# A mixture of experts on lists of its own tokens, in a four-layer kernel on one core

## The chip, the core and the metric

The kernel runs on one NeuronCore of a Trainium2 chip. The metric is device time in microseconds of one execution, lower is better. All arithmetic is in 32-bit floats (some matmul operands are rounded to the fp32r format).

## The reference

Four residual layers on x of shape (4, 512, 128), that is four blocks (batch rows) of 512 tokens. Each layer normalizes its input (layer norm without gain) and adds its result to x.

```python
x = x + attention(ln(x), WQ, WK, WV, WO)     # 16 heads of 8, causal softmax
x = x + moe(ln(x), Wr, W1, b1, W2, b2)       # 8 experts, top 2
x = x + layer1(ln(x), ...)                   # gated linear recurrence and a feed-forward, layer norms inside
x = x + ternary(ln(x), w1, w2, h1, h2, w3)   # weights in {-1, 0, 1}, gelu between

def moe(x):
    xt = x.reshape(T, D)                               # T = 2048, D = 128
    topv, topi = top_k(softmax(xt @ Wr), 2)
    topv = topv / sum(topv)
    onehot = one_hot(topi, 8)
    rank = cumsum(onehot, axis=0)                      # over tokens, for each choice
    keep = (rank <= 320) * onehot                      # capacity int(T * 1.25 / 8)
    w = einsum('tk,tke->te', topv, keep)
    h = gelu(einsum('td,edf->etf', xt, W1) + b1)       # F = 512
    y = einsum('etf,efd->etd', h, W2) + b2
    return einsum('te,etd->td', w, y)
```

The reference computes all eight experts for all tokens and weighs them with w, which is zero for all but two experts of a token.

## The kernel before

A block's 512 tokens are four tiles of 128 (`TB` = 4). x is kept in SBUF as `xs` with tokens on partitions; matmuls take it transposed, `yT` (128 channels by 512 tokens). The stages are Python generators. Each yields after a step the time in us that the step is thought to take on TensorE, and `weave` (L158) merges several generators into one program order: it always continues the stage whose sum of yields, times a factor of the stream, is lowest. Matmuls and transposes (L62, L65) keep that order on TensorE, so a matmul whose operand is late holds up all that follow it there. On the other engines and queues the framework schedules instructions by itself, in an order that respects their dependencies; an engine executes its own list in order.

The work is two stretches a block, after an opening that does the attention of block 0 (L706 to L730). The first (L742 to L752) weaves `experts(b)` (factor 1.0), `feed(b-1)` and `ternary(b-1)` (1.2), and `maxima` of block b+1, the attention's row maxima (2.0); for b = 0, `round_weights`, which loads the ternary weights, rounds them on GpSimd and checks them, stands in for feed and ternary. For b = 4 only feed and ternary of the last block are left. The second (L755 to L763) weaves `recurrence(b)` (1.0) with a chain for the following blocks (0.8): the attention's second pass `second.group`, its `output`, `route(b+1)` and `project(b+2)`. `project` computes queries and keys, stores them to DRAM as `rows_q` and `rows_k` and loads them back spread as `qs` and `ks`, which `maxima` of the next stretch needs.

`route` (L351) computes the router's softmax and the two choices of each token (`oh`, one-hot by tile, choice and expert), counts ranks with matmuls against a triangular matrix (`pr`), applies the capacity, forms w, transposes it (`pw`), copies it (`wT`) and stores it to DRAM (`wd`).

`experts` (L441) runs each expert on all 512 tokens of the block. An expert is four matmuls of 512 columns into `ph`, a Gelu on ScalarE each (`hT`, L467), four matmuls into `py`, a product with the expert's row of w that a DMA has spread over all partitions (`wb`, L459; `yw`, L451), and on GpSimd a sum into `acc` (L452). The bias b2 enters by a matmul with w (`pb2`, L473). `second` of an expert is emitted within the next expert. At the end `acc` is transposed and added to `xs` (L481). `fetch` (L431) loads an expert's weights (`ew`) two experts ahead on the SP queue.

`recurrence` (L487) begins with two layer norms of `xs`, then a projection `pp` for each of 8 channel groups and four weights. `layernorm` (L111) takes four statistics on VectorE and a power on GpSimd (`ln_rs`, L122). In `ternary` (L580) `halves` (L581) splits an activation into a rounded and a residual half; the residual is computed on GpSimd for even indices and on VectorE for odd ones (L585). PSUM banks come from `bank` (L75): two with the tag "pt", shared by nearly all stages, and one "sum".

At the end a value that is nonzero when the ternary weights are not representable (`wide_weights`, L669) decides about a branch (L767) that recomputes the ternary layer in full precision. It is not taken with these inputs.

Of the kernel before, what the change touches and what calls it, by code (L numbers as in the profile page):

```python
# [10 lines left out]
F32 = mybir.dt.float32  # L11
F32R = mybir.dt.float32r
# [23 lines left out]
CAP = max(1, int(NB * S * 1.25 / E))  # L36

# [5 lines left out]
def block_kernel(ctx: ExitStack, tc: tile.TileContext, i: dict, out: bass.AP):  # L43
# [24 lines left out]
    class Turn:  # L68


        tile = ps_d.tile

    turn = Turn()

    def bank(name, tag="pt", shape=(P, S)):  # L75

        return ps_d.tile(list(shape), F32, tag=tag, name=name, bufs=2 if tag == "pt" else 1)
# [51 lines left out]
    def flip(src):  # L129

        pt = turn.tile([P, TB, P], F32, tag="pt", name="pt")
        for t in range(TB):
            transpose(pt[:, t, :], src[:, t, :])
        return pt
# [4 lines left out]
    def normed(src):  # L139
        y = ypool.tile([P, TB, D], F32, tag="y", name="y")  # L140
        layernorm(src, y)
        return y

    def turned(y, gain=None, shift=None):

        yT = ypool.tile([P, S], F32, tag="yT", name="yT", bufs=3)
# [38 lines left out]
    def project(b, big):  # L185
# [25 lines left out]
        pv = turn.tile([P, TB, D], F32, tag="pt", name="pv")  # L211
# [15 lines left out]
    def maxima(g):  # L227
# [27 lines left out]
        pm = turn.tile([P, TB, P], F32, tag="pt", name="pm")  # L255
# [8 lines left out]
    class Weights:  # L264
# [69 lines left out]
        def output(self, b):  # L334
# [6 lines left out]
            pa = turn.tile([P, TB, D], F32, tag="pt", name="pa")  # L341
# [6 lines left out]
    yTs, wTs, wds = {}, {}, {}  # L348
    taken = rt.tile([P, 2 * E], F32, name="taken")

    def route(b):  # L351
# [3 lines left out]
        yT = yTs[b] = turned(y)  # L355
        yield 1.0
        pl = turn.tile([P, TB, E], F32, tag="pt", name="pl")
# [19 lines left out]
        eq = rt.tile([P, TB, E], F32, name="rt_eq", tag="rt_eq")  # L377
        for k in range(2):
# [3 lines left out]
            first = rt.tile([P, TB], F32, name=f"rt_first{k}", tag=f"rt_first{k}")  # L382
            nc.vector.tensor_reduce(first, eq, AX.X, ALU.max)
            nc.vector.tensor_tensor(oh[:, :, k, :], revb, wide(first), ALU.is_equal)
# [13 lines left out]
        for t in range(TB):  # L398
# [6 lines left out]
        rank = rt.tile([P, TB, 2 * E], F32, name="rt_rank", tag="rt_rank")  # L405
        nc.vector.tensor_tensor(
            rank, pr[:, 0:TB, :], taken.unsqueeze(1).to_broadcast([P, TB, 2 * E]), ALU.add
        )
        nc.vector.tensor_tensor(taken, taken, pr[:, TB, :], ALU.add)
        wk2 = rt.tile([P, TB * 2, E], F32, name="rt_wk", tag="rt_wk")  # L410
        nc.vector.scalar_tensor_tensor(
            wk2.rearrange("p n e -> p (n e)"), rank.rearrange("p n k -> p (n k)"), CAP + 0.5,
            ohf.rearrange("p n k -> p (n k)"), ALU.is_le, ALU.mult,
        )
        nc.vector.tensor_tensor(wk2, wk2, wide(tv.rearrange("p n k -> p (n k)")), ALU.mult)
        w = rt.tile([P, TB, E], F32, name="rt_w", tag="rt_w")
        w4 = wk2.rearrange("p (n k) e -> p n k e", k=2)
        nc.vector.tensor_tensor(w, w4[:, :, 0, :], w4[:, :, 1, :], ALU.add)
        yield 3.0
        pw = turn.tile([E, TB, P], F32, tag="pt", name="pw")  # L420
        for t in range(TB):
            transpose(pw[:, t, :], w[:, t, :])
        wT = wTs[b] = rt.tile([E, S], F32, name="wT", tag="wT", bufs=2)
        nc.scalar.copy(wT, pw.rearrange("e t q -> e (t q)"))
        wd = wds[b] = scr.tile([E, S], F32, tag="wd", name="wd")
        nc.sync.dma_start(wd, wT)
# [4 lines left out]
    def fetch(n):  # L431

        if n < NB * E and n not in ews:
            e = n % E
            w1 = ew.tile([P, F], F32, tag="ew1", name="ew1")
            nc.sync.dma_start(w1, i["E1"][e])
            w2 = ew.tile([P, FC, D], F32, tag="ew2", name="ew2")
# [3 lines left out]
    def experts(b, moe):  # L441
        acc = moe.tile([P, S], F32, tag="acc", name="acc", bufs=1)
        late = None

        def second(e, hT, w2, wb):
            py = bank("py", "sum")
            for c in range(FC):
                mm(py, lhsT=w2[:, c, :], rhs=hT[c], start=(c == 0), stop=(c == FC - 1))
            yield 3.44
            yw = moe.tile([P, S], F32, tag="yw", name="yw")  # L450
            nc.vector.tensor_tensor(yw, py, wb, ALU.mult)  # L451
            nc.gpsimd.tensor_tensor(acc, acc, yw, ALU.add)  # L452

        for e in range(E):
# [3 lines left out]
            wb = moe.tile([P, S], F32, tag="wb", name="wb", bufs=2)  # L458
            nc.sync.dma_start(wb, wds[b][e : e + 1, :].to_broadcast([P, S]))  # L459
            fetch(n + 1)  # L460
            fetch(n + 2)
            hT = []
            for c in range(FC):
                ph = bank("ph")
                mm(ph, lhsT=w1[:, ts(c, P)], rhs=yTs[b], start=True, stop=True)
                h = moe.tile([P, S], F32, tag="hT", name="hT", bufs=6)
                nc.scalar.activation(h, ph, AF.Gelu, bias=mb1[:, e * FC + c : e * FC + c + 1])  # L467
                hT.append(h)
                yield 0.86
                if c == 1 and late is None:  # L470

                    pb2 = bank("pb2")
                    mm(pb2, lhsT=mb2, rhs=wTs[b], start=True, stop=True)  # L473
                    nc.vector.tensor_copy(acc, pb2)
                    yield 0.86
                elif c == 1:
                    yield from second(*late)
            late = (e, hT, w2, wb)
        yield from second(*late)
        yield 2.0  # L480
# [99 lines left out]
    def ternary(b, tern):  # L580
        def halves(src, hi, lo, c):  # L581

            nc.vector.tensor_copy(hi, src)  # L583
# [265 lines left out]
```

## Time and profile before

| | |
|---|---|
| device time, median of 3 runs | 934.65 us (932.77 to 938.14) |
| profiled execution, device time | 934.39 us |
| its span in the trace | 932.7 us |
| mean granted TensorE clock | 0.879 |
| TensorE matmul busy | 767.6 us, 82% |
| TensorE weight load busy | 357.8 us, 38% |
| VectorE busy | 410.8 us, 44% |
| ScalarE busy | 308.8 us, 33% |
| GpSimd busy | 173.2 us, 19% |
| DMA | 51.07 MB, mean 55 GB/s |

In the rows of the profile, PE is TensorE, PEld its weight loads, DVE is VectorE, ACT ScalarE, POOL GpSimd, and SPq the DMA queue of SyncE. A row of a group gives line, engine, operation, output and inputs, shapes and count, then busy time in us and the mean of one in ns, then the idle time of its engine ahead of it and what ended that. L63 and L66 are the helpers for all matmuls and transposes, so those rows are told apart by tile names. A 32-bit matmul appears as two records (two weight loads and two passes). Ends of matmuls are modelled, so the durations of consecutive ones overlap; the chain of waits shows how much time a run of them took.

### The profile page before, as it was taken

What the parts mean: (1) busy time and instruction counts of PE and PEld (TensorE: products, weight loads), DVE (VectorE), ACT (ScalarE), POOL (GpSimd) and SP (SyncE); (2) the same over time, 40 slices, a digit from 0 to 9 for tenths busy, and PEclk for the clock granted to TensorE, in tenths of its full rate; (3) what the DMA queues carried; (4) which work ended last, traced back from release to release, by engine and by line L of the source; (5) the groups of instructions that cost most, each with busy time, mean ns of one, the idle gap of its engine ahead of it and who ended that gap; (6) DMA issues with size and microseconds to landing.
All of it is one profiled execution on the core that took longest, in us unless ns stands there. A gap on an engine that the chain in (4) does not pass through costs nothing.

```text
span 932.7 us, 8943 instructions
## 1 busy us (share of the span) xinstructions
PE 767.6 (82%) x3234; PEld 357.8 (38%) x3234; DVE 410.8 (44%) x943; ACT 308.8 (33%) x441; POOL 173.2 (19%) x219
## 2 busy tenths in 40 slices
PE   2367678897998598997998599997998989969776
PEld 1134333443343244553343244453343335523244
DVE  3343054543357436433357326533357143257253
ACT  1013523133542233333542143333643433212212
POOL 3001314513210012222210002122211022200011
PEclk8555969896899799997999699997999999979869
DMA  8600063421000612111000512111000121000000
GB/s 266 176 1 1 1 215 113 139 76 34 1 1 1 210 58 71 45 46 34 1 1 1 203 45 91 46 45 34 1 1 21 48 91 34 12 12 0 1 0 14
DMA packets 47807, 51.07 MB, mean 55 GB/s; under 512 B 6376, under 2 KB 29424, under 8 KB 47760
## 3 DMA queue, kind: packets, MB, share of 16 engines
q1 hardware_dynamic: 47184, 50.21, 17.3%
q8 instruction: 27, 0.44, 0.2%
q10 hardware_dynamic: 576, 0.26, 0.1%
q14 instruction: 20, 0.16, 0.1%
HBM read 40.95 MB, written 9.50 MB: 54 GB/s over the span
## 4 chain that ended last, share of the span: by engine, by line
PE 61%; DVE 15%; DMA 6%; ACT 6%; issue 6%; POOL 4%; SPq 1%; DVEq 0%; ACTq 0%; POOLq 0%
PE ph L63 16%; PE py L63 11%; PE pp L63 10%; PE s L63 7%; PE po L63 4%; PE pt L66 3%; PE por L63 2%; DVE mx L245 2%; POOL ln_rs L122 2%; ACT ex L284 2%; DMA rows_k<-hl 2%; PE pf L63 2%; PE pa L63 2%; DVE ln_st L118 2%; PE pff L63 1%
## 5 line engine op out<-in xcount | busy, mean ns | idle before, releaser
L63 PE MATMUL ph<-yT,ew 128*128 128x512 f32 x256 | 137.4, 641 | 4.1 <-ACT hT L467 1.4
L467 ACT ACTIVATE hT<-ph,w_mb 128x512 f32<-128x512 f32 x128 | 88.0, 688 | 158.7 <-PE ph L63 157.5
L245 DVE TENSOR_REDUCE mx<-s 128x2 f32<-128x1024 f32 (+3 forms) x128 | 97.9, 816 | 93.7 <-PE s L63 93.4
L63 PE MATMUL py<-hT,ew 128*128 128x512 f32 x256 | 118.0, 604 | 0.6 <-DVE yw L451 0.6
L284 ACT ACTIVATE ex<-s 128x768 f32<-128x768 f32 (+1 forms) x96 | 79.4, 879 | 83.3 <-PE s L63 83.1
L452 POOL TENSOR_TENSOR acc<-acc,yw 128x512 f32<-128x512 f32 x32 | 40.7, 1272 | 243.1 <-DVE yw L451 235.5
L289 POOL TENSOR_SCALAR_AFFINE_SELECT ex<-ex 128x256 f32<-128x256 f32 (+1 forms) x96 | 49.1, 516 | 181.9 <-ACT ex L284 181.1
L63 PE MATMUL s<-ks,qs 32*128 32x512 f32 (+3 forms) x256 | 33.6, 457 | 46.0 <-DMA ks<-rows_k 32.1
L63 PEld LDWEIGHTS py<-hT,ew 128*128 128x128 f32 x256 | 48.7, 194 | 57.3 <-issue 53.1
L63 PEld LDWEIGHTS ph<-yT,ew 128*128 128x128 f32 x256 | 43.9, 198 | 51.0 <-ACT hT L467 15.3
L63 PE MATMUL po<-ex,vs 128*32 128x128 f32 (+3 forms) x512 | 57.7, 526 | 6.0 <-POOL ex L289 5.9
L451 DVE TENSOR_TENSOR yw<-py,wb 128x512 f32<-128x512 f32 x32 | 22.1, 690 | 90.0 <-PE py L63 85.9
L63 PE MATMUL ph<-hhh,r_h_w 128*128 128x512 f32 x128 | 58.0, 453 | 1.0 <-ACT h L627 0.8
L63 PE MATMUL ph<-hhl,r_h_w 128*128 128x512 f32 x128 | 51.9, 406 | 0.2 <-DVE hhl L585 0.2
L583 DVE CAST hhh<-h 128x512 fp32r<-128x512 f32 x48 | 21.1, 439 | 63.0 <-ACT h L627 62.7
L63 PEld LDWEIGHTS s<-ks,qs 32*128 32x128 f32 x256 | 16.1, 216 | 82.4 <-issue 28.3
L504 DVE SCALAR_TENSOR_TENSOR kv<-pp,w_bv,k 128x512 f32<-128x512 f32 x32 | 23.9, 747 | 53.6 <-PE pp L63 53.6
L585 POOL TENSOR_TENSOR hhl<-h,hhh 128x512 fp32r<-128x512 f32 x24 | 30.6, 1275 | 90.5 <-DVE hhh L583 88.0
L63 PE MATMUL s<-qs,ks 32*128 32x512 f32 (+3 forms) x256 | 35.2, 455 | 12.8 <-ACT ex L284 8.0
L122 POOL TENSOR_TENSOR ln_rs<-ln_ve,mhalf 128x4 f32<-128x4 f32 x24 | 24.3, 1013 | 103.7 <-DVE ln_ve L121 103.2
L627 ACT ACTIVATE h<-ph,w_h_s 128x512 f32<-128x512 f32 x32 | 22.0, 688 | 65.1 <-PE ph L63 61.5
L506 DVE TENSOR_TENSOR_SCAN st<-dec,kv 128x512 f32<-128x512 f32 x32 | 39.6, 1237 | 0.7
(168 smaller groups left out, 1051.6 us busy)
## 6 DMA issues: line engine op xcount, KB each, us to landing
ew<-in_E_dram SPq DMA_DIRECT2D x64, 256.0 KB, 2.8
wb<-wd SPq DMA_DIRECT2D x32, 256.0 KB, 3.5
rows_q<-hl SPq DMA_DIRECT2D x8, 512.0 KB, 3.3
rows_k<-hl SPq DMA_DIRECT2D x8, 512.0 KB, 4.7
qs<-rows_q SPq DMA_DIRECT2D x16, 256.0 KB, 4.0
ks<-rows_k SPq DMA_DIRECT2D x16, 256.0 KB, 4.1
stage<-in_h_w_dram SPq DMA_DIRECT2D x2, 1024.0 KB, 5.7
xs<-in_x_dram SPq DMA_DIRECT2D x4, 256.0 KB, 4.2
```

The lines of the kernel that those rows point to most:

```text
L63: return tc.keep_in_program_order(nc.tensor.matmul(*args, **kwargs))
L66: tc.keep_in_program_order(nc.tensor.transpose(dst, src, ident))
L122: nc.gpsimd.tensor_tensor(rs, ve, mhalf, ALU.pow)
L245: nc.vector.tensor_reduce(mx[:, t, ts(pr, 2)], pq[pr][:, :, at : at + (t + 1) * P], AX.X, ALU.max, negate=True,)
L284: nc.scalar.activation(ex[:, :, :at], pq[pr][:, :, :at], AF.Exp, scale=scale0)
L289: nc.gpsimd.affine_select(out=e, in_=e, compare_op=ALU.is_ge, fill=0.0, base=0, pattern=[[0, 2], [0, len(part)], [1, P]], channel_multipli ...
L451: nc.vector.tensor_tensor(yw, py, wb, ALU.mult)
L452: nc.gpsimd.tensor_tensor(acc, acc, yw, ALU.add)
L467: nc.scalar.activation(h, ph, AF.Gelu, bias=mb1[:, e * FC + c : e * FC + c + 1])
L504: nc.vector.scalar_tensor_tensor(kv, pv, col(bv), k, ALU.add, ALU.mult)
L506: nc.vector.tensor_tensor_scan(st, col(dec).to_broadcast([P, S]), kv, 0.0, ALU.mult, ALU.add)
L585: eng.tensor_tensor(lo, src, hi, ALU.subtract)
```

## The change

The experts run on lists of their own tokens. A list has 192 rows an expert and block (`SEATS`), 1536 rows in all (`ROWS`), in a DRAM area `xgd` (two of them, for even and odd blocks).

`route` computes for each token and choice its row in the lists. A token beyond a list's 192 rows gets a row in a further area, and a flag (`full`). Eight indirect DMAs on GpSimd's queue (four tiles, two choices) then write the normalized tokens to their rows. The transposes of w, `wT` and its store go; w itself is kept in `wall` for the branch, and the two weights of each token in `wks`.

`experts` loads the lists (`xg`), transposes them in three groups of four tiles into `xT`, and runs each expert on its 192 columns. Two matmuls of the first layer share a bank. b2 is added on VectorE on the way out of PSUM. After every second expert `back` transposes three tiles of results and stores them to `ygd`. At the end eight indirect DMAs on GpSimd's queue fetch each token's two results (`got`), and eight operations on VectorE add them, weighted, to `xs`.

`experts` also stores a copy of `xs` to DRAM (`xad`). If any list was too long, or the ternary weights are not representable, the branch at the end runs the experts in the dense form from that copy, then recurrence, feed and ternary of all blocks. The computation of the branch's condition (`special`) follows the last `route`.

At the start four DMAs on GpSimd's queue write zeros to the lists and to the further areas, and mb2 (the bias b2) is loaded transposed, one element a piece. In `ternary` the residual half is always computed on VectorE.

```diff
@@ route @@
-        yT = yTs[b] = turned(y)
+        yT = turned(y)
...
+        incl = rt.tile([P, TB, 2, E], F32, name="rt_incl", tag="rt_incl")
+        nc.vector.tensor_copy(incl.rearrange("p n k e -> p n (k e)"), pr[:, 0:TB, :])
+        seat = rt.tile([P, TB, E], F32, name="rt_seat", tag="rt_seat")
+        nc.vector.tensor_tensor(seat, incl[:, :, 0, :], incl[:, :, 1, :], ALU.add)
...
+        nc.vector.tensor_tensor(mine, oh, seat.unsqueeze(2).to_broadcast([P, TB, 2, E]), ALU.mult)
+        nc.vector.tensor_reduce(row, mine, AX.X, ALU.add)
+        nc.vector.tensor_scalar(full, row, SEATS + 0.5, None, ALU.is_ge)
+        nc.vector.scalar_tensor_tensor(row, first, -float(SEATS), row, ALU.mult, ALU.add)
...
+        nc.vector.tensor_tensor(away, beyond, row, ALU.subtract)
+        nc.vector.tensor_tensor(away, away, full, ALU.mult)
+        nc.vector.tensor_tensor(row, row, away, ALU.add)
+        at = ats[b] = rt.tile([P, TB, 2], I32, name="rt_at", tag="rt_at", bufs=2)
+        nc.vector.tensor_scalar(at, row, float(SEATS * E - 1), None, ALU.add)
+        for t in range(TB):
+            for k in range(2):
+                put = nc.gpsimd.indirect_dma_start(
+                    xgd[b % 2], bass.IndirectOffsetOnAxis(at[:, t, k : k + 1], 0), y[:, t, :], None,
+                )
+                for x in puts:
+                    tc.declare_no_dep(put.ins, x.ins, reason="a row of its own for each token and choice")
+                puts.append(put)
+        yield 1.0
...
-        pw = turn.tile([E, TB, P], F32, tag="pt", name="pw")
-        for t in range(TB):
-            transpose(pw[:, t, :], w[:, t, :])
-        wT = wTs[b] = rt.tile([E, S], F32, name="wT", tag="wT", bufs=2)
-        nc.scalar.copy(wT, pw.rearrange("e t q -> e (t q)"))
-        wd = wds[b] = scr.tile([E, S], F32, tag="wd", name="wd")
-        nc.sync.dma_start(wd, wT)
@@ experts @@
+        xg = moe.tile([P, NL, D], F32, tag="xg", name="xg", bufs=1)
+        nc.sync.dma_start(xg, xgd[b % 2][0:ROWS].rearrange("(n p) d -> p n d", p=P))
+        nc.sync.dma_start(blk(xad, b), blk(xs, b))
+        yield 4.0
+        xT = moe.tile([P, ROWS], F32, tag="xT", name="xT", bufs=1)
+        for n in range(0, NL, TB):
+            pt = flat(flip(xg[:, n : n + TB, :]))
+            if n % (2 * TB):
+                nc.vector.tensor_copy(xT[:, n * P : (n + TB) * P], pt)
+            else:
+                nc.scalar.copy(xT[:, n * P : (n + TB) * P], pt)
+            yield 0.6
...
+        def second(e, hT, w2):
+            py = bank("py", "sum", (P, SEATS))
+            for c in range(FC):
+                mm(py, lhsT=w2[:, c, :], rhs=hT[c // 2][:, c % 2, :], start=(c == 0), stop=(c == FC - 1))
+            nc.vector.tensor_scalar(oT[:, ts(e, SEATS)], py, mb2[:, e : e + 1], None, ALU.add)
+            yield 1.3
+
+        def back(n, m):
+            po = bank("pto", shape=(P, m - n, P))
+            for j in range(n, m):
+                transpose(po[:, j - n, :], oT[:, ts(j, P)])
+            nc.scalar.copy(og[:, n:m, :], po)
+            nc.sync.dma_start(
+                ygd[b % 2][n * P : m * P].rearrange("(n p) d -> p n d", p=P), og[:, n:m, :]
+            )
+            yield 0.5
...
+            for x in range(FC // 2):
+                ph = bank("ph", shape=(P, 2, SEATS))
+                h = moe.tile([P, 2, SEATS], F32, tag="hT", name="hT", bufs=4)
+                for j in range(2):
+                    c = 2 * x + j
+                    mm(ph[:, j, :], lhsT=w1[:, ts(c, P)], rhs=xT[:, ts(e, SEATS)], start=True, stop=True)
+                for j in range(2):
+                    c = e * FC + 2 * x + j
+                    nc.scalar.activation(h[:, j, :], ph[:, j, :], AF.Gelu, bias=mb1[:, c : c + 1])
+                hT.append(h)
+                yield 0.65
...
+        yield from second(*late)
+        yield 1.0
+        yield from back(*(ROWS // E * x // P for x in (E - 2, E)))
+        yield 4.0
+        got = moe.tile([P, TB, 2, D], F32, tag="got", name="got", bufs=1)
+        for t in range(TB):
+            for k in range(2):
+                nc.gpsimd.indirect_dma_start(
+                    got[:, t, k, :], None, ygd[b % 2],
+                    bass.IndirectOffsetOnAxis(ats[b][:, t, k : k + 1], 0),
+                )
+        yield 6.0
+        for t in range(TB):
+            for k in range(2):
+                x = blk(xs, b)[:, t, :]
+                nc.vector.scalar_tensor_tensor(
+                    x, got[:, t, k, :], wks[b][:, t, k : k + 1], x, ALU.mult, ALU.add
+                )
+        yield 0.5
@@ ternary @@
-            eng = nc.gpsimd if c % 2 == 0 else nc.vector
-            eng.tensor_tensor(lo, src, hi, ALU.subtract)
+            nc.vector.tensor_tensor(lo, h, hi, ALU.subtract)
@@ start @@
+    zeros = rt.tile([P, D], F32, name="zeros")
+    nc.gpsimd.memset(zeros, 0.0)
+    for x in range(2):
+        for dst in (xgd[x][0:ROWS], ygd[x][ROWS:]):
+            nc.gpsimd.dma_start(
+                dst.rearrange("(n p) d -> p n d", p=P),
+                zeros.unsqueeze(1).to_broadcast([P, dst.shape[0] // P, D]),
+            )
-    mb2 = load(wpool, "mb2", i["eb2"], [E, D])
+    mb2 = load(wpool, "mb2", i["eb2"].rearrange("e d -> d e"), [P, E])
@@ second stretch of a block @@
-                if b + 2 < NB:
-                    rest.append(project(b + 2, big))
+                rest.append(project(b + 2, big) if b + 2 < NB else special())
```

## The prediction, made before the changed kernel was run

> **What bounds the kernel now.** I read the windows by stage first. E0 to E3 are the stretches of the experts of block 0 to 3, R0 to R3 those of the recurrence, F is the last block's feed-forward and ternary layers alone. These are the rows of E0, R0, E1, E3 and F.
>
> ```profile
> core 0: us, PE busy (x) PEld busy (x) DVE busy (x) ACT busy (x) POOL busy (x), PEclk, DMA share, GB/s
> 120.30:222.00 101.70, 86.01 (x323) 39.26 (x321) 48.08 (x103) 30.37 (x45) 28.68 (x19) 0.89 0.41 132
> 222.00:317.30 95.30, 78.01 (x408) 32.09 (x408) 46.13 (x130) 38.25 (x54) 18.59 (x30) 0.86 0.11 37
> 317.30:427.50 110.20, 104.42 (x392) 51.87 (x392) 50.82 (x92) 36.09 (x54) 18.86 (x15) 0.97 0.21 64
> 725.40:819.00 93.60, 88.03 (x246) 42.65 (x246) 26.05 (x53) 32.83 (x48) 18.84 (x15) 1.00 0.16 45
> 872.00:932.70 60.70, 42.32 (x120) 24.93 (x120) 21.73 (x48) 13.07 (x19) 9.76 (x9) 0.77 0.02 5
> ```
>
> In E1 PE is busy for 104 of 110 us at nearly full clock: these stretches are bound by PE, with DVE under half. The groups say with what: an expert matmul is two records, and 256 + 256 records are the experts' (busy times of neighbours overlap).
>
> ```profile
> L63 PE MATMUL ph<-yT,ew 128*128 128x512 f32 x256 | 137.4, 641 | 4.1 <-ACT hT L467 1.4 <-DVE acc L474 1.0 <-DMA ew<-in_E_dram 0.7
> L63 PE MATMUL py<-hT,ew 128*128 128x512 f32 x256 | 118.0, 604 | 0.6 <-DVE yw L451 0.6
> ```
>
> The chain of waits, which does not overlap, gives real pitches: eight records (four matmuls) of 512 columns, eight of 128 columns, four transposes, and the DMA pair before E1.
>
> ```profile
> 210.66 0.44 PE pm L66 x4
> 276.04 0.91 PE pa L63 x8
> 309.17 4.69 DMA rows_k<-hl
> 313.93 3.31 DMA ks<-rows_k
> 409.97 3.43 PE py L63 x8
> ```
>
> The timeline shows PE idle before E1 until that DMA lands, and POOL nearly unused before it:
>
> ```profile
> 303.64 1.27 POOL L563 TENSOR_TENSOR xs<-xs,xin 128x512 f32<-128x512 f32 x1 [16.38 <-DVE xin L545]
> 317.29 0.80 PE L63 MATMUL s<-ks,qs 32*128 32x512 f32 x4 [9.61 <-DMA ks<-rows_k]
> ```
>
> Last, the DMA issues (the last number is us to landing) and POOL's smallest arithmetic:
>
> ```profile
> ew<-in_E_dram SPq DMA_DIRECT2D x64, 256.0 KB, 2.8
> stage<-in_h_w_dram SPq DMA_DIRECT2D x2, 1024.0 KB, 5.7
> out_dram<-res SPq DMA_DIRECT2D x4, 256.0 KB, 2.3
> L122 POOL TENSOR_TENSOR ln_rs<-ln_ve,mhalf 128x4 f32<-128x4 f32 x24 | 24.3, 1013 | 103.7 <-DVE ln_ve L121 103.2
> ```
>
> The sum is made against the profiled execution, 934.39 us (span 932.7, 1.7 around it); the median, 934.65, is the same within 0.03%.
>
> **PE work.** A record costs 3.43/8 = 0.429 us at 512 columns and 0.91/8 = 0.114 at 128. On the line between them 192 columns cost 0.166, eight records 1.33. A block has 16 such groups: 21.3 us for 54.9, so 33.6 us less, 134 in four blocks. Added are 24 transposes a block at 0.11 (2.6 us); eight transposes (0.9) and the bias matmul (1.3, at 320.4 in the same chain) go: +0.4. The dropped yw, acc and wb work lay under PE. What is won is then decided by what is late next.
>
> **Is the dense form run?** The reference's own routing on its inputs, computed by hand from its formulas, gives lists of 102 to 160 tokens a block and expert, under 192. So the branch is skipped as before.
>
> **Price of an indirect DMA on POOL.** The trace has none. Below, an SP issue of 0.33 to 0.45 us (the timeline's ew and rows issues); above, a whole small DMA, 2.3 to 2.8 us. I take 1.2 us each, near POOL's own 1.01 us row, the nearest thing that POOL does, and somewhat above it since each names 128 rows. Eight are 9.6 us. Landing after the last: 2.5.
>
> **E0** (before: routing's last matmul ends at 131.5, first recurrence matmul pp of R0 at 239.6). New chain: ten small DVE steps at 0.22 (2.2), eight scatters 9.6, landing 2.5, the 0.79 MB load of the lists 4.8 (between 2.8 and 5.7), three flips with copies 1.5: first expert matmul at 152. PE then has 21.3 + 1.3 transposes + six maxima units of 1.0 + 0.9 = 29.5 us, 33 at clock 0.9: 185. Then copy 0.6, store 2.5, eight gathers 9.6, landing 2.5, last add 0.3 = 15.5; two layernorms 8.3 (427.4 to 436.4 in R1, less the add); flip and copy 2.0 (825.6 to 827.6): pp at 211. **-29 us.** Round_weights' chain of loads and POOL casts (138 to 183 before) starts some 10 us later and still ends about when the gathers begin.
>
> **E1 and E2.** The scatters fill POOL from about 300 to 310. Behind them stand only the add L563 and feed's ln_rs (303.6, 305.0 before); project's ln_rs ran at 286, ahead of them. PE waits for ks until 317 anyway, which is the cover; with none, 9.6 us would be lost. DMA moves 323 to 349 GB/s there (windows 310 to 320), and gets 1.5 MB more (scatters, lists, the copy of xs) less two wb of 0.5 MB: +3 us, first s at 320, first expert matmul after two maxima units and the flips at 324. PE up to the last expert: 21.3 + 2.6 + feed 7.8 + six maxima units and pm 6.9 + half of pa/pb 1.9 = 40.5, 42.6 at 0.95, and 6 of stalls (a flip waits for the copy of the one before): 373. Then only ternary and maxima are left, and PE no longer binds: ternary alone takes 27 us from there in F (898 to 925), DVE in that tail has 27.4 (halves and gelu products 15.5, maxima 9.4, adds 2.4); interleaved I take 31: 404, where 428 was before. **-24 each.** The gathers end at 373 + 15.5, under that tail, so R1's layernorms come earlier; PE has second.group first there, **-2 each.** Without the tail 15.5 + 8.3 us would stand open. POOL's halves go to DVE (0.69 instead of 1.27 us): in the sum of DVE, and F unchanged (its last half was DVE's).
>
> **E3 and R3.** No ks wait and no maxima. Scatters from 718, landed at 730, lists at 734.5, first expert matmul 736.5 (before 720.3). PE stands in order behind the first flip: 16 us idle, then some us at half clock (0.50 in 315:320, 0.91 in 320:325 after the idle time before E1), 2 lost. Work 21.3 + 2.6 + 7.8 + 1.9 + stalls 3 + 2 = 38.6: 775. Ternary alone, 27 as above: 802. Recurrence's input is ready at 775 + 15.5 + 8.3 = 799, so pp starts at 804.6 (flip and copy 2.0) instead of 827.6: **-23.**
>
> **Start.** Zeroing four DRAM areas is 2.62 MB in rows of 512 B while DMA is full (358 to 373 GB/s from 15 to 25 us, first maxima at 27): 7.3 us by bytes; more if each row costs the mean packet's 55 ns (17.3% of 16 x 932.7 us over 47184 packets: 17 us over 16 engines), less where DMA later idles (0.08 at 35:40). I take **+6**, ends 0 and 13. The transposed mb2 is 1024 single elements; dec's 2 KB took 8.7 us to land, but mb2 isn't needed until E0: 0. The larger branch is still jumped over (instruction fetch takes 0.3% of the queues): 0. special() moves a reduction, one matmul and two small DVE steps to the end of R2, under recurrence there: 0, at most 1.
>
> **Sum:** -29 - 26 - 26 - 23 + 6 = -98: **836 us.**
>
> **Rivals.** *Slower: POOL's issue.* If an indirect DMA holds POOL for p us, every us over 1.2 costs 16 in E0, 8 each in E1, E2, E3, and the gathers join where their slack (17 us in E1, 3 in E3) ends. At p = 3.3 the gain is gone (34 + 2 x 17 + 31); at 4 the time is 836 + 45 + 2 x 28 + 42 = 979. For it: scatters that wait for each other would pay 2.3 to 2.8 us apiece; against: they are declared independent. Chance 0.08. DVE's 0.44 us SBUF casts (L583) could hold each gather back by that much, 3.5 us a block, inside the slack. The Trainium skill ("SBUF — State Buffer", section "SBUF: two separate sides") says more: a DMA issued by GpSimd beside a DVE tensor_copy took about 3.1 us instead of 0.62, for want of descriptors; with 3.1 for every one an estimate is 836 + 1.9 x 40 + 12 = 924. No run here shows it yet.
>
> *Chains bind.* The streams are woven for the PE's time, and feed plus ternary need 55 us alone (871 to 926 in F). If experts don't fit between: E1 = 3 + 4 + 24 + 55 + 8 of maxima = 94 instead of 110; with E0 -20, E2 -16, E3 and R3 together -10 (24 + 55 after 736.5, then pp), start +6: 878. For it: DVE and latency hold the tail already in my count; against: F runs its first half at half clock. Chance 0.20.
>
> *All hidden.* p = 0.45 (-12 in E0, -6 in E3), start 0 (-6), tails at ternary's 27 (-8): 804. Chance 0.11.
>
> *Not what it says:* the dense branch runs and repeats experts, recurrence, feed and ternary: four times 55 of expert matmuls, 45 of recurrence (819 to 870 less its start) and 55 as in F, 620 us more. Against it are the lists. 0.01.
>
> **Numbers.** The forecast's case has 0.58, chains 0.20, hidden 0.11, slower 0.09, no change 0.02 (the losses cancel the gain). About 0.5%, 4.7 us, is what a measurement of this kernel can tell from no change. The range: p = 2.5 gives +59 (21 + 10 + 10 + 18), start +7: 902; the low end is 804. Both unknowns at the high end together are unlikely, and the chains' case lies at 878: 804 to 890.
>
> **What would show it.** Right: 0.33 us a 192-column matmul; PE busy about 630 us; E1 near 85 us with its second half full of DVE-released waits; PE in E3 idle 16 us for xT; POOL's indirect rows at 1 to 1.5 us. Wrong: PE waiting for xg beyond ks in E1, gathers that end after ternary, first s later than 40 us, SP holding ks behind the list load.

## The result, and the profile after

The changed kernel takes 902.85 us (median of 4 runs, 899.41 to 905.84) against 934.19 for the kernel before on the same chip (4 runs, 932.77 to 938.14). The ratio is 0.966, 95% interval 0.962 to 0.969: a gain of 31 us where 98 were forecast, outside the range of 804 to 890. The profiled execution has a span of 901.1 us and a granted clock of 0.822 (before 932.7 and 0.879).

The prices of the parts came out as forecast. Two rows of the timeline give the pitch of eight records of 192 columns, 1.31 us (165.50 to 166.81; forecast 1.33), and PE's busy time fell from 767.6 to 647.8 us (forecast 630).

```profile
165.50 1.46 PE L64 MATMUL py<-hT,ew 128*128 128x192 f32 x8
166.81 1.46 PE L64 MATMUL ph<-xT,ew 128*128 128x192 f32 x8
```

The groups of the page show the experts' two kinds of matmul, 256 records each (before 137.4 and 118.0 us busy), and the indirect DMAs on POOL at 0.98 us. With 0.30 us of issue between two of them (a row of the timeline further down) they follow each other every 1.27 us (forecast 1.2). The list load lands in 5.0 us by the DMA issues (forecast 4.8).

```profile
L64 PE MATMUL ph<-xT,ew 128*128 128x192 f32 x256 | 57.3, 359 | 3.4 <-ACT xT L481 1.4
L64 PE MATMUL py<-hT,ew 128*128 128x192 f32 x256 | 49.8, 339 | 10.0 <-DVE xoT L491 10.0
L536 POOL DMA_INDIRECT got<-ygd,rt_at x32 | 31.5, 985 | 86.6 <-DMA ygd<-og 78.1
L434 POOL DMA_INDIRECT xgd<-y,rt_at x32 | 31.3, 977 | 65.4 <-DVE wall L454 26.9
```

```profile
xg<-xgd SPq DMA_DIRECT2D x4, 768.0 KB, 5.0
```

What did not come is the time. The windows by stage show where PE stands idle now: for E0 the wait for the lists, the experts, and the rest up to the recurrence; for E1 the wait for ks, the experts, and the ternary tail; for E3 the experts and the tail.

```profile
core 0: us, PE busy (x) PEld busy (x) DVE busy (x) ACT busy (x) POOL busy (x), PEclk, DMA share, GB/s
136.30:157.00 20.70, 4.82 (x22) 3.00 (x22) 7.73 (x28) 0.00 (x0) 9.76 (x10) 0.50 0.57 181
157.00:205.30 48.30, 39.63 (x217) 33.44 (x217) 20.28 (x32) 16.33 (x40) 16.60 (x8) 0.79 0.48 143
205.30:245.90 40.60, 21.55 (x164) 10.94 (x160) 18.41 (x55) 12.49 (x16) 14.37 (x20) 0.66 0.09 25
301.70:330.30 28.60, 9.56 (x32) 4.75 (x32) 10.26 (x42) 2.44 (x4) 10.12 (x10) 0.70 0.40 136
330.30:383.00 52.70, 44.26 (x258) 33.18 (x259) 22.41 (x45) 20.83 (x47) 1.02 (x1) 0.90 0.41 117
383.00:424.00 41.00, 30.27 (x159) 19.83 (x158) 34.66 (x86) 11.07 (x16) 10.13 (x10) 0.98 0.09 25
717.70:757.70 40.00, 37.01 (x178) 29.11 (x179) 7.34 (x23) 19.64 (x45) 1.01 (x1) 0.93 0.29 81
757.70:797.70 40.00, 30.23 (x100) 19.09 (x98) 27.00 (x69) 9.51 (x14) 9.81 (x10) 0.87 0.07 18
```

Before, E1 had PE busy in 104 of 110 us. Now only the experts' part of E3 is near that (37.0 of 40.0); in E0 and E1 PE is busy for 39.6 of 48.3 and 44.3 of 52.7 us there. In E1's last 41 us DVE is the fullest engine (34.7).

The timeline before E1 shows how POOL's list reaches the ks wait. The eighth put is at 316.39; only then comes `ln_rs` of feed, for which DVE has waited 7.39 us; behind that DVE operation stands `hl` of project, behind it the store of `rows_k` and the load of ks, and PE starts 17.40 us after its last work (9.61 before the change).

```profile
316.39 0.97 POOL L434 DMA_INDIRECT xgd<-y,rt_at  x1 [0.30 <-issue]
317.38 1.05 POOL L121 TENSOR_TENSOR ln_rs<-ln_ve,mhalf 128x4 f32<-128x4 f32 x1
318.47 2.06 DVE L123 TENSOR_SCALAR y<-xin,ln_mv,ln_rs 128x128 f32<-128x128 f32 x4 [7.39 <-POOL ln_rs L121]
320.44 0.68 DVE L198 TENSOR_TENSOR hl<-pqk,hl 128x512 fp32r<-128x512 f32 x1
321.77 1.24 SPq L201 DMA_DIRECT2D rows_k<-hl  x2
330.34 0.80 PE L64 MATMUL s<-ks,qs 32*128 32x512 f32 x4 [17.40 <-DMA ks<-rows_k]
```

For the account I cut the span at the first recurrence matmul pp of each block. The forecast's column follows from its own terms (239.6 + 6 - 29 = 217 and so on).

| us | before | forecast | after |
|---|---|---|---|
| start to pp of R0 | 239.6 | 217 | 245.9 |
| to pp of R1 (R0, E1) | 208.5 | 182.5 | 195.5 |
| to pp of R2 (R1, E2) | 211.3 | 185.3 | 200.7 |
| to pp of R3 (R2, E3) | 168.2 | 145.2 | 155.6 |
| to the end (R3, F) | 105.1 | 105.1 | 103.4 |

28.9 us of the missing 66 are in E0, 13.0 in E1, 15.4 in E2, 10.4 in E3; the end takes 1.7 less. Where a time below is "after routing", it is counted from the start of routing's rank matmuls `pr`.

### The profile page after: what moved, and what is told of

The parts are those of the page before. It is cut to its first block, busy times and chain, and to the rows that moved or that the text cites. A ratio compares the mean times of both kernels' runs of the same rounds, so it can differ in the third digit from the quotient of the medians.

```text
span 901.1 us, 9226 instructions
## 1 busy us (share of the span) xinstructions
PE 647.8 (72%) x3290; PEld 368.3 (41%) x3290; DVE 424.3 (47%) x1050; ACT 276.4 (31%) x461; POOL 169.7 (19%) x233
## 5 line engine op out<-in xcount | busy, mean ns | idle before, releaser
L121 POOL TENSOR_TENSOR ln_rs<-ln_ve,mhalf 128x4 f32<-128x4 f32 x24 | 24.7, 1030 | 251.1 <-DVE ln_ve L120 251.0
L64 PE MATMUL ph<-hh,r_h_w 128*128 128x512 f32 x128 | 56.8, 444 | 5.8 <-DVE hh L683 4.6
L64 PE MATMUL ph<-xT,ew 128*128 128x192 f32 x256 | 57.3, 359 | 3.4 <-ACT xT L481 1.4
L64 PE MATMUL ph<-hl,r_h_w 128*128 128x512 f32 x128 | 55.3, 432 | 4.0 <-DVE hl L684 3.2
L64 PE MATMUL py<-hT,ew 128*128 128x192 f32 x256 | 49.8, 339 | 10.0 <-DVE xoT L491 10.0
L521 ACT ACTIVATE hT<-ph,w_mb 128x192 f32<-128x192 f32 x128 | 45.8, 417 | 33.9 <-PE ph L64 32.4
L64 PEld LDWEIGHTS ph<-xT,ew 128*128 128x128 f32 x256 | 45.9, 208 | 11.5 <-ACT hT L521 4.8
L536 POOL DMA_INDIRECT got<-ygd,rt_at x32 | 31.5, 985 | 86.6 <-DMA ygd<-og 78.1
L434 POOL DMA_INDIRECT xgd<-y,rt_at x32 | 31.3, 977 | 65.4 <-DVE wall L454 26.9
L491 DVE TENSOR_SCALAR xoT<-py,w_mb 128x192 f32<-128x192 f32 x32 | 13.3, 415 | 58.7 <-PE py L64 58.7
L64 PEld LDWEIGHTS s<-qs,ks 32*128 32x128 f32 x256 | 17.7, 220 | 49.9 <-ACT ex L283 26.2
```

The lines of the kernel that those rows point to most:

```text
L64: return tc.keep_in_program_order(nc.tensor.matmul(*args, **kwargs))
L121: nc.gpsimd.tensor_tensor(rs, ve, mhalf, ALU.pow)
L434: put = nc.gpsimd.indirect_dma_start(xgd[b % 2], bass.IndirectOffsetOnAxis(at[:, t, k : k + 1], 0), y[:, t, :], None,)
L491: nc.vector.tensor_scalar(oT[:, ts(e, SEATS)], py, mb2[:, e : e + 1], None, ALU.add)
L521: nc.scalar.activation(h[:, j, :], ph[:, j, :], AF.Gelu, bias=mb1[:, c : c + 1])
L536: nc.gpsimd.indirect_dma_start(got[:, t, k, :], None, ygd[b % 2], bass.IndirectOffsetOnAxis(ats[b][:, t, k : k + 1], 0),)
```

## The experiments

Theory: the parts have their forecast price, but PE's order and the lists of DVE and POOL were laid out for dense experts, so the stretches now end with waits. Rivals: the indirect DMAs' price on POOL; PE's work after all; DVE's added halves. The first eight runs are edits of the changed kernel (902.9). The runs were made on several chips, on which the kernel before took 932.6 to 934.6 us by the median. What is said of a stretch comes from one profiled execution of each kernel.

**The weight of the maxima**

```diff
-    streams.append((chain(*(maxima(g) for g in range(NG))), 2.0))
+    streams.append((chain(*(maxima(g) for g in range(NG))), 1.1))
```

> Only the weight of the maxima stream in the order of the program changes, 2.0 to 1.1, so that the four groups of maxima are laid among the experts' matmuls and not behind them. Theory (order): a maxima unit takes both score banks and waits for DVE's reductions, about 9.5 us a group when nothing else is left for PE; E0 runs about 1.7 groups alone after the last expert matmul, so E0 falls by 10 to 16 us, E1 and E2 by 4 to 10 each: 868 to 888 us. Rival (price of the indirect DMAs on POOL decides): the last expert comes later, the gathers with it, and the time is 900 to 912. By the forecast's price, 1.0 us of PE a unit, the order of equal work changes nothing: 899 to 907.

905.8 us (901.3 to 906.6): no gain, a miss for the theory as I had it. The time lies in the bands of the rival and of the forecast, and as the rival said the last expert of E0 ends later (73.2 us after routing, 68.8 without) and the first get comes 4.5 us later. In E0 the last transposes pm came at 209.4 instead of 228.6, and yet pp only 2.4 us earlier. The timeline of that kernel says why:

```profile
214.05 1.00 POOL L536 DMA_INDIRECT got<-ygd,rt_at  x1 [19.56 <-ACT ex L283]
227.75 0.41 POOL L288 TENSOR_SCALAR_AFFINE_SELECT ex<-ex 128x256 f32<-128x256 f32 x1
228.22 1.92 PE L64 MATMUL po<-ex,vs 128*32 128x512 f32 x4 [12.95 <-POOL ex L288]
```

The next block's exponentials began at 212, but their masks stand on POOL behind the eight gets and a layer norm, so PE waits 12.95 us. In E1 and E2 the experts ended later, and the tail was all ternary.

**The flip of the lists later in PE's order**

```diff
     nc.sync.dma_start(blk(xad, b), blk(xs, b))
-    yield 4.0
+    yield 14.0
```

> Only the place of the first flip of the lists changes: the experts' first yield is 14.0 instead of 4.0, so that more maxima units, feed and stage work stand ahead of it on PE. Theory (order): PE stood 28.0 us in all for the lists' load at the first flip; most of that is filled in E0 (12.7) and E3, but what moves ahead of the flip pushes the experts back, so 885 to 897. Rival (the load of the lists itself is the path, since all that follows needs the gathers): 900 to 910.

888.2 us (886.8 to 890.0), as the theory expected. PE's wait for xg (28.0 us in all) is gone. The windows of E1 and E3 (experts, then tail) show 26.2 and 21.4 us behind the last expert, where it had been 40 and 38 (to ternary's flip).

```profile
344.60:391.20 46.60, 39.70 (x253) 32.20 (x251) 30.85 (x62) 19.36 (x46) 1.02 (x1) 1.00 0.35 98
391.20:417.40 26.20, 19.74 (x102) 14.01 (x99) 19.61 (x52) 6.95 (x10) 8.78 (x9) 0.93 0.14 38
711.20:753.00 41.80, 35.50 (x192) 29.54 (x191) 18.98 (x43) 19.36 (x45) 1.01 (x1) 1.00 0.28 78
753.00:774.40 21.40, 15.72 (x60) 10.66 (x59) 11.83 (x33) 4.50 (x7) 8.85 (x9) 0.92 0.13 34
```

Experts that start later leave PE to feed and ternary first, so ternary's first matmuls run before the last expert (366.4 against 391), not behind it. But the last expert also ends later, 11.5 us in E1 and 10.5 in E3, counted from routing. From pp to pp the gain is 3.3 us in E0, 4.5 in E1, 7.7 in E2, and only 0.8 in E3, where the shorter tail is paid for ahead of it.

**The projection ahead of the routing**

```diff
     rest = [second.output(b + 1), route(b + 1)]
-    rest.append(project(b + 2, big) if b + 2 < NB else special())
+    if b + 2 < NB:
+        rest.insert(1, project(b + 2, big))
+    else:
+        rest.append(special())
```

> Only the order of two stages at the end of R0 and R1 changes: the projection of block b+2 goes ahead of the routing of block b+1, so its layernorm, its halves and its row copies no longer stand behind the eight puts and the routing on POOL, DVE and SP. Theory (order): the wait for ks before E1 and E2 (17.4 us before E1, against 9.6 before the change) falls by 5 to 8 us each, the puts come about 8 us later under the maxima: 886 to 896. Rival (DMA bandwidth holds the ks rows): the wait stays, 899 to 906.

891.1 us (889.9 to 894.3), as expected. Then both edits together:

> The late flip of the lists (first yield 14.0) and the projection ahead of the routing, together. Alone they gave 888.2 and 891.1 us against 902.9. Theory (order; two different waits, for the lists and for ks): the gains add, 26 us: 874 to 881. Rival (one idle time before E1 and E2, whose two ends they shorten): the better of the two remains, 885 to 891.

860.3 us (859.4 to 862.9), ratio to before 0.923 (0.919 to 0.926): 42.6 us less, where the single gains make 26.4, and so beyond the bands of both theory and rival. The chains of waits of PE (total, times, longest) say why they add to more than their sum. In the changed kernel, then with the projection first:

```profile
PE s L64 <- DMA ks<-rows_k: 56.9, 4, 19.6
PE pt L67 <- DMA xg<-xgd: 28.0, 4, 12.7
```

```profile
PE pt L67 <- DMA xg<-xgd: 52.4, 4, 13.9
PE s L64 <- DMA ks<-rows_k: 21.4, 2, 19.2
```

and with both:

```profile
PE s L64 <- DMA ks<-rows_k: 21.6, 2, 20.5
```

The projection alone took 35 us from the ks wait and gave 24 back at the flip, which stood next in order. With the flip late as well, little is left but the opening's 21.6 (the wait for xg is 0.8).

**Plain transfers in place of the indirect ones**

```diff
-    for t in range(TB):
-        for k in range(2):
-            put = nc.gpsimd.indirect_dma_start(xgd[b % 2], ...)
+    for k in range(2):
+        nc.gpsimd.dma_start(xgd[b % 2][k * S : (k + 1) * S].rearrange(...), y)
...
-    for t in range(TB):
-        for k in range(2):
-            nc.gpsimd.indirect_dma_start(got[:, t, k, :], ...)
+    for k in range(2):
+        nc.gpsimd.dma_start(got[:, :, k, :], ...)
```

> The eight puts and the eight gets of a block are replaced by two plain transfers each from POOL's queue, of the same bytes in token order, so the lists hold other rows than the reference's; all other work is the same. Rival (price of the indirect DMAs): if POOL's issue is where the 66 us missing from the forecast went, 835 to 850. Theory (order): the puts cost where something stands behind them, about 6 us in E0 and 5 us each before E1, E2 and in E3, and the gets are hidden under the ternary tail except in E0: 876 to 892. By the forecast's own terms, eight puts at 1.2 us on the path in E0 and E3 and eight gets in E0 and E3 make 25 to 33 us: 870 to 878.

871.3 us (861.3 to 873.8): 32 us less. That is a gain some us beyond the theory's band and in line with the forecast's own terms for the puts and gets, which the forecast had already paid; the 66 us are not there. In the profiled execution (861.3 us, the shortest) the lists came 12.5 us after E0's routing instead of 20.7, and E3's tail takes 30.9 us instead of 38.0. This second gain is no term of the forecast's, which had E3's gets under ternary with 3 us to spare.

**Half of the second matmul**

```diff
-    for c in range(FC):
-        mm(py, ..., start=(c == 0), stop=(c == FC - 1))
+    for c in range(FC // 2):
+        mm(py, ..., start=(c == 0), stop=(c == FC // 2 - 1))
```

> The experts' second matmul leaves out half of its contraction (two of four chunks), so PE has 8 x 4 records of 192 columns fewer in a block: at 1.30 us for eight records 5.2 us a block, 20.8 in all; order, DVE, ACT and POOL work stay. Forecast's view (the experts' part is bound by PE's work): the time falls by most of it, 882 to 888. Theory (chains of waits set the stretches): a third of it or less, 895 to 903.

887.8 us (885.0 to 889.9): 15 of the 20.8 us come out, within the band of the forecast's view, a miss for the theory. From the first expert matmul to the end of the last the four blocks take 39.3, 39.2, 39.2 and 32.8 us, where it had been 45.3, 42.3, 45.1 and 37.4. So PE's work still sets the experts' own part; in E1 to E3 the missing time lies ahead of that part and behind it.

**Short reductions**

```diff
-    mx[:, t, ts(pr, 2)], pq[pr][:, :, at : at + (t + 1) * P], AX.X, ALU.max,
+    mx[:, t, ts(pr, 2)], pq[pr][:, :, at : at + P], AX.X, ALU.max,
```

> Every maxima reduction on DVE reads only the first 128 columns of its scores, the rest is left out; matmuls, order and waits stay. DVE has about 14 us less in each of the start, E0, E1 and E2. Forecast's price of a maxima unit (1.0 us of PE, the reductions under PE's work): the start falls by some us, E0 to E2 by 0 to 3 each, 890 to 900. Theory (a unit is matmuls, then reductions, then the next unit's matmuls on the same two banks, and DVE is the full engine of E1's and E2's tails): E0 by 5 to 12, E1 and E2 by 5 to 10 each, the start by 5 to 10: 862 to 883.

878.7 us (873.8 to 882.9), 24 less, within the theory's band; pp of R0 comes 14.7 us earlier (8.7 of them in the opening), E1 and E2 gain 3.4 and 6.1 (for E1 the theory had at least 5). So the reductions have a price beside PE's.

**The halves back on POOL**

```diff
-    nc.vector.tensor_tensor(lo, h, hi, ALU.subtract)
+    eng = nc.gpsimd if c % 2 == 0 else nc.vector
+    eng.tensor_tensor(lo, h, hi, ALU.subtract)
```

> The low halves of the ternary operands of even index go back to POOL (1.27 us instead of DVE's 0.69), as before the change; nothing else. Theory (DVE is at 85% in the tails of E1 to E3): 4 us of DVE less in each tail, 2 to 4 us a stretch, 892 to 899. Rival (POOL's list is in order, and the gathers stand in it ahead of the halves in the tails): PE waits for halves behind gathers, 905 to 920. Forecast's price of this edit: nothing, 900 to 906.

906.9 us (901.4 to 909.6): the theory's gain of 4 to 11 us did not come. The median is 4 us up, in the rival's band and just above the forecast's, but the runs with and without the edit overlap. The rival's mechanism is there in small: one half of E1's tail stands between two gets on POOL, PE waits 3.6 us in all for halves of POOL, and the tails of E1 to E3 take 43.9, 44.0 and 40.0 us (40.4, 40.9 and 38.0 without).

The next runs look into E0. Where nothing else is said, they are edits of the kernel with both changes of order (860.3).

**The check of the weights later**

```diff
     nc.gpsimd.tensor_tensor(w, w, rw[key], ALU.subtract)
+    yield 4.0
     nc.vector.tensor_reduce(odd[:, n : n + 1], w, ...)
-    yield 3.0
```

> On the same kernel (860.3 us), the reduction that ends each step of the weights' rounding stands one yield later in the program, so that DVE does not wait for POOL's subtraction in E0 (9.6, 5.2, 2.5 and 2.1 us of DVE waiting there in the changed kernel). Theory (DVE's list holds back the maxima and the experts' bias adds): the last expert of E0 comes 3 to 6 us earlier, the time falls by 1 to 5, 855 to 859. Rival (nothing behind those waits is on the path): 859 to 862.

861.2 us (857.8 to 865.5); the last expert of E0 begins 69.3 us after routing, 69.4 without the edit. But the edit did not take the waits away. These are DVE's waits for the subtraction without it, then with it:

```profile
DVE odd L756 <- POOL stage L755: 21.9, 5, 10.1
```

```profile
DVE odd L757 <- POOL stage L755: 20.9, 5, 9.6
```

So the run does not test the theory. That the waits are not on the path isn't shown, and the traces speak against it: PE's longest wait for a bias add in E0 is 7.8 us without the edit and 7.0 with it, and that add stands on DVE behind the reduction.

**The kernel before with the projection first**

> The kernel before, with nothing but the order of project(b+2) and route(b+1) turned. It says what the order is worth to the dense form. Theory (in the dense form the ks wait is 9.6 us idle before E1 and E2 too): 5 to 8 us from each, 918 to 925. Rival (PE's work bounds E1 and E2 there, the idle time only moves to the wait for routing's weights): 930 to 936.

917.2 us (916.4 to 920.3), ratio 0.982 (0.980 to 0.983). The order was worth 17 us to the dense form too, a little more than the theory had. With that order in both, lists take 917 to 891, and with the late flip to 860.

**Gathers behind the masks**

```diff
-    streams = [(recurrence(b, big), 1.0)]
+    streams = [(chain(gather(b, big, 4.0), recurrence(b, big)) if b == 0 else recurrence(b, big), 1.0)]
```

with the gathers and adds of `experts` as a stage `gather` of their own, and weight 1.1 for block 1's maxima.

> On the kernel with the late lists and the projection first (860.3 us), E0 alone is changed: its maxima are laid early (weight 1.1), and its gathers are issued in R0, behind the first scores and masks of the next block's attention, and no longer ahead of them in POOL's list. Theory (E0 and R0 together end with the chain second groups, output, projection, routing, about 80 us from the first free mask, and that mask stood at 227 us behind the eight gathers): masks free at about 214, routing's last matmul of block 1 at 294 to 298 instead of 307.4, in all 848 to 853. Rival (recurrence's input sets R0): the gathers come later, 859 to 866.

875.1 us (874.0 to 878.7), slower, and a badly made experiment: with the flip at 14.0 the early maxima went ahead of it, the lists were flipped 40.8 us after routing (26.2 without), and the first five gets still stood ahead of the masks on POOL. It doesn't tell the theories apart. The next one takes the masks from POOL.

**Masks by matmul in E0, and in all blocks**

```diff
     product(pq, spread, mTs[g], t * P, S, at)
+    if g < self.by_pe:
+        for h in range(NG):
+            mm(pq[h // 2][:, h % 2, at : at + P], lhsT=identb, rhs=mask_k, ...)
...
-    nc.gpsimd.affine_select(out=e, in_=e, ...)
+    if g >= self.by_pe:
+        nc.gpsimd.affine_select(out=e, in_=e, ...)
```

Here `by_pe` is 2 for block 1 and 0 else; the flip's first yield is 4.0 in E0 and 14.0 else, the maxima's weight 1.1 in E0.

> On the kernel with the late lists and the projection first (860.3 us), only E0 and R0 change: the lists are flipped early there (first yield 4.0), the maxima laid early (weight 1.1), and the first two groups of block 1's second attention pass get their causal mask by a matmul ahead of the exponential, so that they don't wait for POOL behind the eight gathers. Theory (E0 ends where the second pass starts, and R0 is a fixed 80 us from there to routing's last matmul, 77 to 82 in six traces): with early maxima the first exponential is at 76 us after block 0's routing instead of 87, and nothing holds its masks, so block 1's routing comes at 294 to 298 instead of 307, 847 to 852 in all. Rival (the recurrence's input, behind the gathers, is the end of E0): 858 to 863.

854.5 us (853.1 to 859.1), ratio 0.915 (0.911 to 0.918): the best time here. But the theory's reason fell. The second pass started at 212, and block 1's routing came 95 us later, not 80. What had looked like a fixed time from the first mask was one from pp. The timeline shows the new end of E0, the recurrence's input:

```profile
234.00 1.24 PE L67 MATMUL pt<-ident,y 128*128 128x128 f32 x4 [4.41 <-DVE y L129]
238.28 2.04 PE L64 MATMUL pp<-yT,w_lk 128*128 128x512 f32 x2 [1.17 <-DVE o L322]
```

That is 27 us after the last expert, gathers and layer norms included, as the forecast had it (25.8). The profiled spans of this kernel and of the one with both edits are 856.9 and 857.3, so where its last 6 us by the medians come from isn't shown. In these two executions E0 is 6.8 us shorter from routing to pp, and R0 from there to the next routing is 4.0 longer. With all groups:

> The same with the masks of all groups of blocks 1 to 3 by matmul: 64 short matmuls more on PE in each of R0, R1 and R2, about 5 us a stretch by the maxima's mask rows (0.62 us for eight), and no wait of PE for POOL in the second pass. Theory (R is a chain score, exponential, mask, values, with PE idle in its waits): R falls by 2 to 6 us each against the one with masks in E0 alone, 832 to 848. Rival (R is bound by PE's work): R grows by up to 5 each, 852 to 866.

873.0 us (871.1 to 875.2). From pp to the next routing R0, R1 and R2 take 72.1, 68.0 and 56.8 us, against 69.0, 65.0 and 53.7 with masks in E0 alone. That is 3.0 us more in each, so the rival was right that R grows with PE's work. Its band ended at 866: half of the 18.5 us lies outside these stretches and isn't explained.

**No maxima in E0** (on the changed kernel)

```diff
-    if b + 1 < NB:
+    if 0 < b < NB - 1:
         streams.append((chain(*(maxima(g) for g in range(NG))), 2.0))
```

> The changed kernel without the row maxima of block 1 in E0 (its second pass uses block 0's); all else stays. In the changed kernel the experts of E0 take 46.8 us from the first flip to the last expert matmul, where the forecast had 33 with six maxima units at 1.0 us, and the recurrence's first matmul comes 42 us after the last expert. Forecast's price (1.0 us a unit, 6.9 with pm): the last expert 7 us earlier. Theory (a unit costs its wait for DVE on the two banks, about 2 us among the experts, and the chain of the rest holds PE's order up to the recurrence's flip): the last expert 11 to 15 us earlier, the recurrence's first matmul 26 to 30 us after it, E0 85 to 90 us instead of 109.5, in all 878 to 884. Rival (a small clock and the experts' own chains stretch E0): the last expert 3 to 7 us earlier, E0 96 to 102 us, 889 to 896.

887.3 us (885.1 to 892.4). Counted from routing the last expert comes 8.3 us earlier and pp 14.3 us (E0 95.2 us). It lies between the two accounts. Of the 14.3 us the forecast had paid 6.9 for the maxima, so they explain some 7 of the 29 us by which E0 missed it. What is left are the experts, 35.9 us from their first matmul to their last where the forecast would have 26 (33 less 7 for the maxima), and PE's wait for POOL behind the gets:

```profile
214.90 1.92 PE L64 MATMUL po<-ex,vs 128*32 128x512 f32 x4 [12.96 <-POOL ex L288]
```

## Why the prediction was wrong

**Right:** that it is faster, the price of the matmuls, the puts, gets and list load, the opening (+6.4 for +6), that the branch isn't run, the first expert matmul of E0 and E3 (23.4 and 24.7 us after routing; 22.1 and 23.5 forecast), E3's last expert (61.9 us after routing; 62). In E1 and E2 the gathers lie under ternary, as forecast. That p = 2.5 in the sum gives 902, the measured time, is chance: 1.27 was measured.

**Wrong: the tails.** The step that failed is "half of pa/pb" in E1 and "Ternary alone, 27" in E3. 27 us was F from the middle of pa/pb on. I put half of pa/pb among the experts; PE's order has all of it behind them:

```profile
381.55 1.57 PE L64 MATMUL py<-hT,ew 128*128 128x192 f32 x8 [1.30 <-DVE xoT L491]
382.82 0.53 PE L64 MATMUL pa<-yTh,r_w_w 128*128 128x512 f32 x1
```

From the first pa to the flip at the end ternary alone takes 32.4 us (F of the changed kernel, 861.6 to 893.9), with maxima beside it 40.7 (E1). The term 31 measured 40.4 in E1, 27 measured 38 in E3. The late flip shows the mechanism: with pa/pb ahead of the last expert the tails are 26 and 21.

In E3 the order is about half of it. From the last expert to the middle of pa/pb are 5.3 us; from there to the flip it is 32.7 where F had 27. Ternary's part from the first `ph` to the flip takes 28.2 us, and 20.9 in F:

```profile
767.58:795.79 28.21, 23.45 (x72) 15.57 (x73) 18.34 (x55) 5.50 (x8) 8.56 (x9) 0.82 0.07 19
872.99:893.94 20.95, 19.49 (x73) 14.63 (x73) 12.03 (x21) 5.51 (x8) 0.00 (x0) 0.91 0.01 2
```

In E3 the adds of the gathers and the recurrence's layer norms stand among ternary's halves on DVE (18.3 us busy, 12.0 in F), PE waits 3.7 us for halves there, 0.5 in F, and the clock is lower. With plain transfers the adds come before the halves, and the same part takes 21.2 us. So the gathers lie under ternary in time, but what DVE does with them was put at nothing beside ternary in E3.

**Wrong: the start of E1 and E2.** "+3" measured +6.7 for the first s, and "4" from there to the first expert matmul measured 10.5: the two maxima units with their waits for DVE take 4.8 us, PE's wait for xg 2.1 (a wait that the prediction had named as a sign of being wrong), the flips and their copies 3.6. The prediction named the queue, POOL's `ln_rs` behind the scatters, and gave PE's wait for ks as its cover. The cover was the wrong way round: project's `hl` stands on DVE behind that layer norm, so the puts lengthen the wait for ks. Against this the experts' part took 42.3 us for 49 forecast. E2 splits in the same way: 7.1 for "+3", 9.7 for "4", 45.1 for 49 and 40.9 for 31.

**Wrong: E0, by all of its 29 us.** Two terms. The experts' 33 us measured 45.5, with PE busy 39.6 of 48.3 us (flips included) at a clock of 0.79: the maxima unit, priced at 1.0 us of PE, takes DVE's reductions too before the next unit can use the two banks. And the check of the ternary weights was put at nothing on DVE. Its reduction `odd` waits there for POOL's subtraction, and the bias add that frees the bank of `py` stands behind both; PE's longest wait among the experts ends with that add:

```profile
186.79 2.29 DVE L756 TENSOR_REDUCE odd<-stage 128x1 f32<-128x2048 f32 x1 [5.23 <-POOL stage L755]
189.00 1.94 DVE L244 TENSOR_REDUCE mx<-s 128x2 f32<-128x512 f32 x4
190.85 0.41 DVE L491 TENSOR_SCALAR xoT<-py,w_mb 128x192 f32<-128x192 f32 x1
191.32 2.92 PE L64 MATMUL py<-hT,ew 128*128 128x192 f32 x8 [4.37 <-DVE xoT L491]
```

The 25.8 us from the last expert to pp measured 40.6. The gets and layer norms took their time (y is done at 231.6), but PE had the second pass ahead of the flip, and that began with the last maxima:

```profile
228.63 1.09 PE L67 MATMUL pm<-ident,mh 128*128 128x128 f32 x4 [3.75 <-DVE mh L252]
232.75 0.42 POOL L288 TENSOR_SCALAR_AFFINE_SELECT ex<-ex 128x256 f32<-128x256 f32 x1 [2.29 <-ACT ex L283]
243.46 0.66 PE L67 MATMUL pt<-ident,y 128*128 128x128 f32 x4
```

Taking the maxima from E0 gives 14.3 us back, 6.9 of them their own price in the forecast, and taking the masks from POOL with early maxima leaves 27 us after the last expert. Without the maxima the experts still take 35.9 us for 26. The trace shows the same order there: the check's reduction, 3.74 us behind POOL, holds back a bias add, PE waits 4.15 us for it, and half clock follows (below). How much the check costs in all stays open, for no run took it away.

**The rivals.** "Chains bind" was nearest in its mechanism. Of its 94 us for E1, 3 lie ahead of the first s; these measured 6.7, and the other 91 measured 93.2 (first s to ternary's flip), so that its -16 became -10 in E1, and the same in E2 (from pp to ternary's flip). Its -10 for E3 and R3 measured -12.6. It too had -20 in E0, where nothing came, and so its time, like the forecast's and the hidden case's, lay too low. POOL's issue at 3.3 us did not come: 1.27. DVE casts beside the gets held them back by 0.25 us at most: in E1's tail, with copies of L683 at 392.35, 395.15 and 398.08, the eight gets were busy 0.95 to 1.20 us each.

```profile
392.66 0.97 POOL L536 DMA_INDIRECT got<-ygd,rt_at  x1 [0.30 <-issue]
395.19 1.20 POOL L536 DMA_INDIRECT got<-ygd,rt_at  x1 [0.30 <-issue]
```

The Trainium skill ("SBUF — State Buffer", section "SBUF: two separate sides") gives some 3.1 us for a DMA issued by GpSimd beside a DVE tensor_copy; no get took that long beside these casts of 0.4 us.

## What to carry to other kernels

When a change shrinks the work of one stream among several that are merged in a fixed order, price the order again: look at which matmul stands next behind the last one of the shrunk stream, and which stages no longer overlap with it. An operation on an idle engine is cheap in itself, but read what is queued behind it on that engine and follow this to the next wait, also when that wait seems to cover it. Two waits in a row on one engine should be removed together: here the first, removed alone, handed two thirds of its time to the second.

## What the hardware showed

A wait costs more than its length. After 4.37 us without work PE ran eight records of 192 columns in 2.92 us instead of 1.46, as the timeline of the changed kernel has it:

```profile
191.32 2.92 PE L64 MATMUL py<-hT,ew 128*128 128x192 f32 x8 [4.37 <-DVE xoT L491]
```

Its windows show the granted clock (the number before the last two) at 0.50 for 8.3 us, though PE was busy for most of them:

```profile
191.30:195.50 4.20, 3.46 (x11) 2.95 (x12) 1.31 (x5) 0.00 (x0) 1.87 (x2) 0.50 0.42 131
195.50:199.60 4.10, 4.07 (x14) 3.15 (x12) 0.00 (x0) 1.79 (x4) 0.00 (x0) 0.50 0.38 108
199.60:203.00 3.40, 2.68 (x17) 1.94 (x16) 2.23 (x2) 0.73 (x2) 0.00 (x0) 0.83 0.21 77
```

PE was busy for 7.5 of these 8.3 us; at full clock that work would take half as long, so an estimate of what is lost beside the wait itself is some 4 us. By the mean of 0.83 in the third window full clock came back at about 200.8, that is 9.4 us after the wait's end and 5.6 us after a gap of 0.72 us in PE's work at 195.2. The Trainium skill ("TensorE: Matmul & The Clock Gate", section "Part 1: The HAM clock gate") has full clock back after about 3.4 us of sustained work; both times here are longer, and what the gap did isn't shown by itself. The mean clock of the changed kernel, 0.822 against 0.879, fits its longer waits; no run varied the clock by itself.
